# Second band of the first image: direct convolution or minimal filtering form in the prelude

## The chip, the cores and the metric

One Trainium2 chip, one core of it. The metric is the device time of one execution in microseconds, as the median of several runs. A core has TensorE (PE, matrix products into the PSUM banks), VectorE (DVE), ScalarE (ACT), GpSimd (POOL) and SyncE (SP, which here only issues transfers). Each engine works its own queue in order; between engines there are only semaphores.

## What is computed

The input is four images of 64x64 points with 128 channels. Two layers follow each other. In the first, `elu(x)` goes through a 3x3 convolution of 128 to 128 channels, then a 3x3 convolution of 128 to 256, whose halves are combined:

```
c1 = conv_same(jax.nn.elu(x), W1, b1)
c2 = conv_same(c1, W2, b2)
a, b = jnp.split(c2, 2, axis=-1)
c3 = a * jax.nn.sigmoid(b)
```

On `c3` there is a causal attention over the 4096 points with keys of 4 and values of 16 channels ("first attention"); its result, projected by W3, is added to c3 and x. The second layer normalizes each point, does a full attention with 16 heads of 8 channels over the 4096 points ("second attention"), then a feed-forward part and a mixture of two of eight experts. All is float32.

## The kernel before

**Units.** An image is cut into 8 chunks of 512 points (8 image rows) and 4 bands of 16 rows, a band being two chunks. The second attention is a stream of steps: a step takes 128 keys of 4 heads against 512 queries, four score matmuls into two PSUM tiles `s` of 128x1024, two exponentials `e` on ScalarE, and four value matmuls into `acc`. There are three tiles `s`, one bank `acc` and one bank `m` for all other work.

**Order of the work.** The program is written out by Python generators, and what they yield decides the order on each engine; `InOrder` (L104) fixes it as written. Two loops do this. `run_alone` (L1261) is the prelude: it takes one piece of each generator in turn: `convolutions` (L536), `first_attention` (L673), `second_operands_beside` (L832), `fold_and_spread` (L1486) and `spread_beside` (L1497). It ends when the second operands of the first two chunks are there, three tap sets are spread and the first image's two bands are past (`not st.plain`, L1505). After that the main loop lays one attention step per turn, of 1.81 us by the planner's costs, and fills TensorE's rest with pieces of the other generators ("fillers"), while the credit of a turn allows it. The planner's costs are constants in the program.

**The first image's stream.** Its segments come in three groups (`plan`, L1383 on): those that need the operands of 2 chunks (64 steps), of 4 chunks (192 steps) and of all 8. A group cannot start before `batches[b].second`, the count of chunks whose second operands are made, has reached its n; until then no step is written. A chunk's second operands (`second_operands`, L749) are: two projections of the first attention's sums with a division, a normalization (whose power is on GpSimd), a transposition, and the q, v and k projections, each through one bank and written to DRAM; keys and values are read back from there.

**Two forms of the convolution.** The direct form (`first_bands`, L484) takes nine matmuls of 128x512 for each chunk and 128 output channels, one for each tap, accumulated in the bank `m`. The minimal filtering form (`winograd`, L437) makes an output tile of 2x2 from sums of inputs: `row_terms` (L425, four GpSimd operations of 128x528 from a band into `r`) and `col_terms` (L431, one GpSimd operation of 128x1024 for each of four columns, into `v`). For each of the four columns there are then four matmuls of 128x256 with spread taps, in two banks; the first bank is copied out to `sd` (by ScalarE in the prelude, by VectorE later), its halves are added and subtracted (`sums`, `sd`), and the second bank is combined with these. `sd` and `sums` have one buffer each. The spread taps `f_wino1` and `f_wino2` are made in the prelude, by VectorE and, for the gate's half of W2, by GpSimd.

**The bands.** `e_band` holds elu(x) and `c_band` the first convolution's result, two of each, 18 rows with one row of the neighbours on each side. In the first image, bands 0 and 1 go through the direct form, by the loop `for r in range(2)` (L502); bands 2 and 3, and all of the later images, through the minimal filtering form (`jobs`, L612). The direct taps for the gate's half lie in the tile `r`, which `row_terms` takes later (L1296).

Of the kernel before, what the change touches and what calls it, by code (L numbers as in the profile page):

```python
# [9 lines left out]
FP = mybir.dt.float32  # L10
FR = mybir.dt.float32r
AF = mybir.ActivationFunctionType
ALU = mybir.AluOpType
AX = mybir.AxisListType

P = 128
C = 128
IMG = 64
N = IMG * IMG
NT = N // P  # L20
QB = 512
# [105 lines left out]
def fast_path(ctx: ExitStack, tc: tile.TileContext, a: dict, where: dict, out: bass.AP, verdict):  # L127
# [7 lines left out]
    x = a["x"]  # L135
    B = x.shape[0]
    pe, act, sp = (InOrder(tc, e) for e in (nc.tensor, nc.scalar, nc.sync))
# [46 lines left out]
    dve, pool = InOrder(tc, nc.vector, dve_time), InOrder(tc, nc.gpsimd, pool_time)  # L184
# [4 lines left out]
    wk = ctx.enter_context(tc.tile_pool(name="f_wk", bufs=2))  # L189
# [9 lines left out]
    def m_tile():  # L199
        return ps_m.tile([P, QB], FP, tag="m", name="m")  # L200
# [7 lines left out]
    def chunk(tag, name=None):  # L208
        return wk.tile([P, QB], FP, tag=tag, bufs=CHUNKS.get(tag, 1), name=name or tag)
# [10 lines left out]
    def bank():  # L220
        return s_tile()[:, :QB] if alone[0] else m_tile()
# [10 lines left out]
    def load_x(b, c, tag):  # L232
        t = chunk(tag)
        sp.dma_start(out=by_k(t), in_=tb_x[b][:, 4 * c : 4 * c + 4, :])
        return t


    wino1 = const.tile([P, 16, C], FP, name="f_wino1")
    wino2 = const.tile([P, 16, 2 * C], FP, name="f_wino2")

    def row_tile():
        return wk.tile([P, 4 * 8 * (IMG + 2)], FP, tag="r", bufs=1, name="r")

    def taps(src, room=None):

        t = wk.tile([P, 3, 3, C], FP, tag="vg", name="taps") if room is None else room
        for i in range(3):
            act.dma_start(out=t[:, i], in_=src[i].rearrange("kw i o -> i kw o"))
        return t
# [7 lines left out]
    taps1 = taps(a["L0_conv_W1"])  # L257
# [8 lines left out]

    e_band = [const.tile([P, 18, IMG + 2], FP, name=f"f_e_band{i}") for i in range(2)]
    c_band = [const.tile([P, 18, IMG + 2], FP, name=f"f_c_band{i}") for i in range(2)]
    for band in (*e_band, *c_band):
        pool.memset(band[:, :, 0:1], 0.0)  # L270
        pool.memset(band[:, :, IMG + 1 :], 0.0)
    pool.memset(e_band[0][:, 0, :], 0.0)
    pool.memset(c_band[0][:, 0, :], 0.0)

# [63 lines left out]
    def transposed(src, ps):  # L338
        for k in range(4):
            pe.transpose(ps[:, k * P : (k + 1) * P], src[:, k * P : (k + 1) * P], ident)  # L340
# [48 lines left out]
    def rows(ap):  # L389
        return ap.rearrange("p (h w) -> p h w", w=IMG)  # L390
# [4 lines left out]
    COLS = (1, 2, 0, 3)  # L395

    spread_of = []
# [27 lines left out]
    def row_terms(band):  # L425
        r = row_tile().rearrange("p (i y x) -> p i y x", i=4, y=8)
        for i, (x, y, op) in enumerate(SUMS):
            pool.tensor_tensor(r[:, i], band[:, x : x + 15 : 2, :], band[:, y : y + 15 : 2, :], op)
        return r

    def col_terms(r, j):  # L431
        v = wk.tile([P, 4, 8, IMG // 2], FP, tag="v", bufs=4, name="v")
        x, y, op = SUMS[j]
        pool.tensor_tensor(v, r[:, :, :, x : x + 63 : 2], r[:, :, :, y : y + 63 : 2], op)
        return v.rearrange("p i y x -> p i (y x)")
# [45 lines left out]
            late.pop(0)()  # L481
            yield 0.0, "free" if late else "stop"

    def first_bands(st, elu):  # L484


        def nine(taps, band, y, n):
            ps = rows(m_tile()[:, : n * IMG])
            for m in range(9):
                i, j = divmod(m, 3)  # L490
                pe.matmul(
                    ps,
                    lhsT=taps[:, i, j, :],
                    rhs=band[:, y + i : y + i + n, j : j + IMG],
                    start=m == 0,
                    stop=m == 8,
                )
                if m in (2, 5):
                    yield 0.0, "stop"
            return ps  # L500

        for r in range(2):  # L502
            here, there = e_band[r], e_band[1 - r]
            c_here = c_band[r]
            if r == 1:
                pool.tensor_copy(c_here[:, 0, :], c_band[0][:, 16, :])
            for band, y, n, to in (
                (here, 0, 8, slice(1, 9)),
                (here, 8, 8, slice(9, 17)),
                (there, 0, 1, slice(17, 18)),  # L510
            ):
                ps = yield from nine(taps1, band, y, n)
                act.activation(c_here[:, to, 1 : IMG + 1], ps, AF.Identity, bias=b1)
                yield 0.0, "stop"
            st.c3 = wk.tile([P, 2 * QB], FP, tag="c3", bufs=2, name="c3")
            inputs = elu(5 + 2 * r)
            for h in range(2):
                c3, gate = st.c3[:, h * QB : (h + 1) * QB], chunk("sd", "gate")
                ps = yield from nine(taps2a, c_here, 8 * h, 8)
                act.activation(rows(c3), ps, AF.Identity, bias=half_b2a, scale=0.5)  # L520
                next(inputs, None)
                yield 0.0, "stop"
                ps = yield from nine(taps2b, c_here, 8 * h, 8)
                act.activation(rows(gate), ps, AF.Tanh, bias=half_b2[:, 1:2], scale=0.5)
                dve.scalar_tensor_tensor(c3, gate, 1.0, c3, ALU.add, ALU.mult)
                st.done.append(c3)
                next(inputs, None)
                yield 0.0, "stop"
            yield from inputs
        st.plain = False  # L530

    def tiles(ap):

        return ap.rearrange("p (y i) (x h) -> p i y x h", i=2, h=2)

    def convolutions(b, st):  # L536
        xs = list(first_x) if b == 0 else [load_x(b, c, "xe") for c in range(2)]
        yield 0.0, "stop"
        made = [0]

        def elu(n):

            todo = range(made[0], n)
            made[0] = max(made[0], n)
            neg, pos = {}, {}
            for at in range(len(todo) + 2 if todo else 0):
                a_, b_, c_ = (todo[i] if 0 <= i < len(todo) else None for i in (at, at - 1, at - 2))
                if b_ is not None:

                    pos[b_] = chunk("pos")  # L550
                    dve.tensor_scalar(pos[b_], xs[b_], 0.0, None, ALU.max)
                    dve.scalar_tensor_tensor(pos[b_], neg[b_], 1.0, pos[b_], ALU.min, ALU.add)
                    if b_ + 2 < NQ:
                        xs.append(load_x(b, b_ + 2, "xe"))
                if a_ is not None:
                    neg[a_] = chunk("neg")
                    act.activation(neg[a_], xs[a_], AF.Exp)
                if c_ is not None:
                    r, k = divmod(c_, 2)
                    ps = bank()  # L560
                    transposed(pos[c_], ps)
                    put = [(r, slice(1 + 8 * k, 9 + 8 * k), slice(0, 8))]
                    if k == 0 and r > 0:
                        put.append((r - 1, slice(17, 18), slice(0, 1)))
                    if k == 1 and r < 3:
                        put.append((r + 1, slice(0, 1), slice(7, 8)))
                    for band, to, of in put:
                        dve.tensor_scalar(
                            e_band[band % 2][:, to, 1 : IMG + 1], rows(ps)[:, of], -1.0, None, ALU.add
                        )  # L570
                yield (0.0 if c_ is None else 0.6), "free" if at == 0 else "stop"
# [40 lines left out]
        jobs = [(0, 0), (0, 1), (0, 2), (1, 0), (0, 3), (1, 1), (1, 2), (1, 3)]  # L612
        yield from elu(3)
        if b == 0:
            yield from first_bands(st, elu)
            jobs = [(0, 2), (0, 3), (1, 2), (1, 3)]
            while len(spread_of) < 3:
                yield 0.0, "wait"
            yield from elu(7)
        else:  # L620
            pool.memset(e_band[0][:, 0, :], 0.0)
        r_ = row_terms(e_band[jobs[0][1] % 2])
        v = [col_terms(r_, j) for j in COLS]
        yield 0.0, "stop"
        for n, (layer, r) in enumerate(jobs):
# [17 lines left out]
            if layer == 0:  # L643
                yield from winograd(wino1, slice(0, C), v, b1, used, first(r))
                here, above = c_band[r % 2], c_band[(r - 1) % 2]
# [18 lines left out]
            v = ahead  # L664
# [622 lines left out]
    for _ in range(3):  # L1287
        next(batches[0].conv)
    taps2a = taps(a["L0_conv_W2"][:, :, :, :C])
    b1 = const.tile([P, 1], FP, name="f_b1")  # L1290
    act.dma_start(out=b1, in_=a["L0_conv_b1"].unsqueeze(1))
    b2 = const.tile([P, 2], FP, name="f_b2")
    act.dma_start(out=b2, in_=a["L0_conv_b2"].rearrange("(h p) -> p h", p=P))
    half_b2 = const.tile([P, 2], FP, name="f_half_b2")
    half_b2a = half_b2[:, 0:1]
    taps2b = taps(  # L1296
        a["L0_conv_W2"][:, :, :, C:], row_tile()[:, : 9 * C].rearrange("p (i j o) -> p i j o", i=3, j=3)
    )
    for _ in range(2):
        next(batches[0].conv)  # L1300
# [201 lines left out]
    st = batches[0]  # L1502
# [87 lines left out]
    ps = m_tile()  # L1590
# [5 lines left out]
    ps = m_tile()  # L1596
# [703 lines left out]
```

## Time and profile before

| what | us |
|---|---|
| median of 3 runs | 7942.97 (7942.77 to 7944.63) |
| profiled execution | 7943.24 |
| its span | 7941.4 |
| ScalarE busy in the span | 7662.2 |
| TensorE busy in the span | 7753.8 |
| VectorE, GpSimd busy | 4804.7, 671.3 |
| ScalarE's first stream exponential | 159.93 |
| ScalarE without a gap from | 179.05 |

How to read the profile: times are from the start of the span. Nearly all instructions are at L114, since a helper records them, so they are told apart by their tiles: `e<-s` is an exponential, `s<-qx,f_kx` scores of the second attention, `m<-f_e_band,taps` a direct matmul of the first convolution, `m<-v,f_wino` (or `s<-v,f_wino`) one of the minimal filtering form. A float32 matmul has two records. In a timeline a line gives start, length from the first to the last of its instructions, engine, operation, count, and in brackets how long the engine had been idle and what released it. A busy TensorE is modelled, and need not be TensorE at its peak.

### The profile page before, as it was taken

Reading aid. Unit: us, or ns where it says so; the run is one execution under the profiler, and the core shown is the slowest. Engines: PE = TensorE matmul, PEld = TensorE weight load, DVE = VectorE, ACT = ScalarE, POOL = GpSimd, SP = SyncE. Lnnn points to the kernel's source line nnn. Section 1 sums busy time; section 2 is a strip of 40 time slices with the busy share of each in tenths; the row PEclk is TensorE's granted clock in tenths of the full one; section 3 lists DMA queues with packets and bytes.
Section 4 is the critical chain, followed back from the end, with each engine's and each line's share of the span. In section 5 each row is a group of like instructions: output and inputs, shape, how many; then the busy total and the mean of one; then the engine's idle time right before and its main releaser. Section 6 shows DMA issues by size and latency. Waiting matters only on the chain.

```text
span 7941.4 us, 237872 instructions
## 1 busy us (share of the span) xinstructions
PE 7753.8 (98%) x103661; PEld 3284.0 (41%) x103661; DVE 4804.7 (61%) x9290; ACT 7662.2 (96%) x8460; POOL 671.3 (8%) x592
## 2 busy tenths in 40 slices
PE   8999999999999999999999999999999999999998
PEld 3333444444444444444444444444444333333334
DVE  5333556463577666656656776665666666666664
ACT  2999999999999999999999999999999999999996
POOL 2201211000021100000002211000000000000000
PEclk9999999999999999999999999999999999999998
DMA  2112011101100111101010011111111111111221
GB/s 89 62 65 69 24 59 45 59 30 57 35 29 25 39 42 52 44 22 44 27 39 26 26 41 39 52 44 34 32 33 49 49 54 51 50 51 50 73 71 37
DMA packets 334835, 360.96 MB, mean 45 GB/s; under 512 B 148212, under 2 KB 224468, under 8 KB 333780
## 3 DMA queue, kind: packets, MB, share of 16 engines
q1 hardware_dynamic: 329763, 343.87, 13.7%
q8 instruction: 814, 13.34, 0.7%
q10 hardware_dynamic: 4016, 1.77, 0.1%
q14 instruction: 242, 1.97, 0.1%
HBM read 209.50 MB, written 136.05 MB: 44 GB/s over the span
## 4 chain that ended last, share of the span: by engine, by line
PE 44%; issue 2%; DVE 2%; ACT 2%; DMA 0%; POOL 0%; SPq 0%; ACTq 0%; DVEq 0%; POOLq 0%
PE acc L114 22%; PE s L114 13%; PE m L114 9%; ACT e L114 2%; DVE ey L114 1%; DVE h L114 0%; DVE em L114 0%; DVE t L114 0%; DVE eg L114 0%; DVE by_e L114 0%; POOL rs L114 0%; ACT th L114 0%; DVE f_c_band L114 0%; DVE c L114 0%; DMA blocks<-d_y 0%
## 5 line engine op out<-in xcount | busy, mean ns | idle before, releaser
L114 ACT ACTIVATE e<-s 128x1024 f32<-128x1024 f32 x8256 | 7600.8, 1118 | 85.6 <-PE s L114 79.8
L114 PE MATMUL acc<-e,vg 128*9 128x128 f32 (+3 forms) x61840 | 4277.8, 387 | 1.9 <-DVE at L114 1.8
L114 PE MATMUL s<-qx,f_kx 32*128 32x512 f32 (+1 forms) x16512 | 2557.6, 494 | 81.1 <-ACT e L114 59.9
L114 PEld LDWEIGHTS acc<-e,vg 128*9 128x9 f32 x61840 | 1563.0, 90 | 1773.8 <-issue 1206.4
L114 PEld LDWEIGHTS s<-qx,f_kx 32*128 32x128 f32 (+1 forms) x16512 | 1054.3, 182 | 2061.6 <-ACT e L114 1339.7
L114 DVE SCALAR_TENSOR_TENSOR ey<-ey,eg 128x512 f32<-128x512 f32 x1344 | 940.9, 700 | 31.9
L114 DVE COPY at<-acc 128x512 f32<-128x512 f32 x131 | 90.5, 691 | 575.4 <-PE acc L114 572.8
L114 PE MATMUL m<-v,f_wino 128*32 128x256 f32 x5376 | 420.2, 391 | 11.7 <-POOL v L114 7.3
L114 DVE TENSOR_SCALAR ey<-m 128x512 f32<-128x512 f32 x448 | 307.6, 687 | 90.3 <-PE m L114 79.3
L114 DVE SCALAR_TENSOR_TENSOR eg<-em,ey 128x512 f32<-128x512 f32 x448 | 317.0, 708 | 11.4
L114 DVE SCALAR_TENSOR_TENSOR ey<-ey,em 128x512 f32<-128x512 f32 x448 | 316.7, 707 | 9.6
L114 POOL TENSOR_TENSOR rs<-ve,f_minus_half 128x4 f32<-128x4 f32 x64 | 65.2, 1019 | 2989.5 <-DVE ve L114 2957.0
L114 DVE SCALAR_TENSOR_TENSOR ey<-eg 128x512 f32<-128x512 f32 x448 | 312.8, 698 | 0.0
L114 DVE COPY sd<-m 128x512 f32<-128x512 f32 x168 | 115.9, 690 | 307.5 <-PE m L114 307.0
L114 POOL TENSOR_TENSOR v<-r 128x1024 f32<-128x1024 f32 x112 | 219.0, 1961 | 968.0 <-PE m L114 967.5
L114 PE MATMUL m<-f_we,y2T 128*32 128x256 f32 x3968 | 291.9, 388 | 0.0
L114 DVE TENSOR_TENSOR by_e<-m,gates 128x512 f32<-128x512 f32 x248 | 170.3, 687 | 178.9 <-PE m L114 177.8
L114 PE MATMUL m<-hT,f_fw 128*32 128x256 f32 (+1 forms) x2728 | 233.1, 390 | 1.3 <-DVE hT L114 1.2
L114 POOL TENSOR_TENSOR t<-t,h 128x512 f32<-128x512 f32 x32 | 44.4, 1389 | 2243.4 <-DVE h L114 2243.4
L114 DVE TENSOR_TENSOR t<-m,t 128x512 f32<-128x512 f32 x61 | 42.2, 691 | 308.7 <-PE m L114 308.7
L114 DVE TENSOR_SCALAR em<-ey 128x512 f32<-128x512 f32 x448 | 200.4, 447 | 13.7
L114 DVE TENSOR_SCALAR em<-em 128x512 int32<-128x512 int32 x448 | 196.1, 438 | 10.0
(262 smaller groups left out, 4382.6 us busy)
## 6 DMA issues: line engine op xcount, KB each, us to landing
f_kx<-d_k SPq DMA_DIRECT2D x139, 512.0 KB
qx<-d_q SPq DMA_DIRECT2D x152, 256.0 KB
d_q<-two SPq DMA_DIRECT2D x64, 512.0 KB
d_a<-at SPq DMA_DIRECT2D x128, 256.0 KB
vg<-d_v SPq DMA_DIRECT2D x32, 576.0 KB
d_k<-two SPq DMA_DIRECT2D x32, 512.0 KB
d_v<-vc SPq DMA_DIRECT2D x32, 288.0 KB
xe<-in_x_dram SPq DMA_DIRECT2D x32, 256.0 KB
```

The costliest lines, as they stand in the source:

```text
L114: made = op(*args, **kw)
```

## The change

The loop over two bands becomes two generators. `first_band` does band 0 as before, except that the ELUs of chunks 3 and 4 are taken between the first convolution's matmul groups and the first half of layer 2, and that row terms and column terms of band 1 are made by GpSimd after the first half of band 0. `second_band` takes band 1 through `winograd` twice for layer 2 and once for layer 1; row 17 of its first convolution stays direct. Between the two layers it makes the row and column terms of `c_band[1]`. It waits for the three spread tap sets before layer 2. `st.plain` is cleared after layer 2; the ELUs of chunks 5 and 6, which were made during band 1, now come after that. The direct gate taps move from the tile `r` to `c_band[1]`, whose side columns are cleared later for that reason.

```diff
-    for band in (*e_band, *c_band):
+    for band in (*e_band, c_band[0]):
+        clear_sides(band)
...
+    def first_band(st, elu):
+        band, c_to = e_band[0], c_band[0]
+        inputs = elu(5)
+        for here, y, n, to in (
+            (band, 0, 8, slice(1, 9)),
+            (band, 8, 8, slice(9, 17)),
+            (e_band[1], 0, 1, slice(17, 18)),
+        ):
+            ps = yield from nine(taps1, here, y, n)
+            act.activation(c_to[:, to, 1 : IMG + 1], ps, AF.Identity, bias=b1)
+            next(inputs, None)
+            yield 0.0, "stop"
...
+            if h == 0:
+                for _ in inputs:
+                    pass
+                made = row_terms(e_band[1])
+                st.terms = [col_terms(made, j) for j in COLS]
+            yield 0.0, "stop"
+
+    def second_band(st, elu, first, second):
+        here = c_band[1]
+        clear_sides(here)
+        pool.tensor_copy(here[:, 0, :], c_band[0][:, 16, :])
+        yield from winograd(wino1, slice(0, C), st.terms, b1, lambda q: None, first(1))
+        ps = yield from nine(taps1, e_band[0], 0, 1)
+        act.activation(here[:, 17:18, 1 : IMG + 1], ps, AF.Identity, bias=b1)
+        made = row_terms(here)
+        v = [col_terms(made, j) for j in COLS]
+        yield 0.0, "stop"
+        while len(spread_of) < 3:
+            yield 0.0, "wait"
+        st.c3 = wk.tile([P, 2 * QB], FP, tag="c3", bufs=2, name="c3")
+        yield from winograd(wino2, slice(0, C), v, half_b2a, lambda q: None, second(1, False))
+        yield from winograd(wino2, slice(C, 2 * C), v, b2[:, 1:2], lambda q: None, second(1, True))
+        st.done += [st.c3[:, :QB], st.c3[:, QB:]]
         st.plain = False
+        yield from elu(7)
...
         if b == 0:
-            yield from first_bands(st, elu)
+            yield from first_band(st, elu)
+            yield from second_band(st, elu, first, second)
             jobs = [(0, 2), (0, 3), (1, 2), (1, 3)]
-            while len(spread_of) < 3:
-                yield 0.0, "wait"
-            yield from elu(7)
...
     taps2b = taps(
-        a["L0_conv_W2"][:, :, :, C:], row_tile()[:, : 9 * C].rearrange("p (i j o) -> p i j o", i=3, j=3)
+        a["L0_conv_W2"][:, :, :, C:],
+        c_band[1].rearrange("p y x -> p (y x)")[:, : 9 * C].rearrange("p (i j o) -> p i j o", i=3, j=3),
     )
```

## The prediction

> **What bounds the kernel now.** I read the page's busy times first, then busy time by stage, then the timelines of ScalarE and TensorE wherever ScalarE stands still.
>
> ```profile
> PE 7753.8 (98%) x103661; PEld 3284.0 (41%) x103661; DVE 4804.7 (61%) x9290; ACT 7662.2 (96%) x8460; POOL 671.3 (8%) x592
> ...
> L114 ACT ACTIVATE e<-s 128x1024 f32<-128x1024 f32 x8256 | 7600.8, 1118 | 85.6 <-PE s L114 79.8
> ```
>
> 8,256 exponentials of 128x1024. Their mean of 1118 ns counts overlap; their pace is 58.30 us for 64 in the ScalarE timeline from 179.05, 0.91 us each. The stages say where ScalarE is not full (columns: window, length, then busy PE, PEld, DVE, ACT, POOL, clock, DMA share, GB/s):
>
> ```profile
> 0.00:156.00 156.00, 134.50 (x486) 65.48 (x486) 76.89 (x179) 24.34 (x35) 27.40 (x56) 1.00 0.31 94
> 156.00:180.00 24.00, 12.88 (x88) 4.93 (x88) 15.83 (x33) 8.71 (x10) 13.68 (x10) 0.72 0.06 22
> 180.00:324.00 144.00, 139.13 (x1616) 49.86 (x1612) 54.51 (x104) 144.00 (x159) 21.48 (x22) 1.00 0.25 84
> 324.00:334.00 10.00, 4.73 (x40) 1.24 (x40) 0.84 (x2) 1.44 (x3) 9.92 (x7) 0.66 0.04 6
> 334.00:700.00 366.00, 360.76 (x4244) 133.93 (x4248) 136.08 (x301) 366.00 (x404) 33.65 (x30) 1.00 0.18 60
> 700.00:724.00 24.00, 13.47 (x172) 5.63 (x168) 5.96 (x15) 13.59 (x16) 0.00 (x0) 0.79 0.52 167
> ```
>
> The prelude runs to about 156 and TensorE carries it. From 180 on ScalarE carries all, except for two holes, at 324 and at 704. So the time is: when ScalarE becomes continuous, plus its work still open then, plus its holes. The two holes in TensorE's timeline:
>
> ```profile
> 321.43 0.50 PE L114 MATMUL s<-qx,f_kx 32*128 32x512 f32 x4
> 329.27 1.08 PE L114 MATMUL m<-v,f_wino 128*32 128x256 f32 x8 [7.34 <-POOL v L114]
> ...
> 703.03 1.06 PE L114 MATMUL acc<-e,vg 128*9 128x256 f32 x24
> 714.13 0.80 PE L114 MATMUL s<-qx,f_kx 32*128 32x512 f32 x4 [10.04 <-DMA f_kx<-d_k]
> ```
>
> At 703 the stream of attention steps has used up the key blocks of chunks 0 to 3 (256 steps) and needs chunk 7's keys, made just before.
>
> **The change, part by part.**
>
> *TensorE in the second band.* Removed: four times nine matmuls of 128x512 for layer 2 and twice nine for layer 1, 7.96 us for nine (the row at 108.65, two records a matmul), 47.8 us in all. Added: 48 matmuls of 128x256, 0.44 us each (the four of q projection, 1.10 us at 79.58, hold as much), 21.1 us. 26.7 us less on TensorE. But they now form chains.
>
> *The chain in place of it.* I followed the changed kernel's built order from 78.75, where the first band's last gate lands on VectorE, with durations from this trace.
> 1. VectorE up to the second normalization: its listed operations sum to 31.2 us (row pitch: projection set 2.57, normalization 1.89, key set 1.56, three two-term sets of 3.05, here two, 128x256 sums 0.34, bank reads 0.35 and 0.61). Waits on TensorE, GpSimd's power (1.15) and exponentials add some 5. It ends at 115.0. The first layer's band is written at 112.0; row 17 is earlier.
> 2. GpSimd is in order: the power (1.02, as at 112.00) stands before the row terms. Rows 5.17 us (at 155.28), first column term 2.0: 116.1 + 7.2 = 123.3. Nothing of layer 2 can start earlier; TensorE's transposes and projections of chunk 1 queue behind its first matmul.
> 3. Eight steps of layer 2. Each is a bank copy on ScalarE 0.66, sum and difference 0.75, two bank reads 0.80, hand-overs 0.1: 2.3 us, because `sd` and `sums` have one buffer. 18.6 us. Chunk 1's operands lie between on VectorE: 8.2 us. First matmul and last gate: 5. So 123.3 + 31.8 = 155.1: hardly before today, where the last gate is on VectorE at 155.95 to 157.13.
>
> Here a rule speaks against the change. First the row: while GpSimd made terms,
>
> ```profile
> 159.81 0.92 DVE L114 TENSOR_SCALAR w<-u,f_consts 128x512 fp32r<-128x512 f32 x1
> 160.77 2.29 DVE L114 SCALAR_TENSOR_TENSOR qx<-u,f_consts,w 128x512 fp32r<-128x512 f32 x1
> ```
>
> against 0.48 and 0.75 at 56.85 and 57.36, yet the bank read xt (163.37, 0.61) is not longer. The Trainium skill, "SBUF — State Buffer", section "SBUF: two separate sides", says that the pair of ports shared by VectorE and GpSimd is an exclusive lock for a whole instruction, for VectorE operations with two SBUF inputs or in a two-port mode. By the rule, some six operations in my window 123 to 129 wait up to a 2.0 us GpSimd instruction each, +8; by the row, five operations lost 5.2 us in all, and fewer of mine fall inside. I take +2: the stream's first projection starts at 156 to 157 and the first exponential at 157.0. Bounds: -6 (lock never met, early waits hidden) to +8.
>
> *Input terms of the second band.* 13 us of GpSimd, from about 46.5 to 60. GpSimd is idle there until 67 (33.49 us before its memset at 67.27), apart from the bias addition of chunk 0's x, now behind them, at 61 instead of 32.5; its reader is at 61.89. Cost 0; if late by a few us, TensorE's w3f at 71.78 is the next reader, so up to 9 us are covered. The ELUs of chunks 3 and 4 move ahead by one to two matmul groups: the same instructions. The tap tile in c_band[1] moves two memsets and a copy to GpSimd at about 86, 0.7 us, in its idle time.
>
> *What is left undone at 157.* Today, ScalarE is continuous from 179.05 and has by then done 8 exponentials of the stream (7.3), six of chunk 2's first attention (4.9) and two ELU exponentials (1.2): 13.5 us. In the changed kernel these come after 157.0, so the same state is reached at 170.5. At the start, TensorE is slow and the single bank m makes it wait for VectorE's projections of chunk 2; the slow start at 175.95 to 179.05 cost 1.16 us of idle, at 161 to 165 2.6; I take 3 (1 to 6). Gain: 179.05 - 173.5 = 5.5 us.
>
> *The hole at 324.* In the built order two more attention steps now lie between the last layer 1 matmul and the first layer 2 matmul (a segment begins there). Two steps are 3.64 us more cover for the same term making: gain 3.6 (0 to 3.6).
>
> *The hole at 704.* Chunks 2 and 3's first attention and projections are done in the stream now. Everything behind them slips by about 20 steps: chunk 3's keys at step 47 of the 64 that the first segments have (30 before), so no wait there; but chunk 7 is not ready at step 256. In the built order, at that point there follow, without a single stream step between, chunk 7's eight first-attention rounds and all its second operands. The rounds are work ScalarE has anyway; only 1.5 us idle ahead of them. The rest is serial:
> - exponential to copied sums 2.0 (148.19 to 150.21); two projections with their divisions 1.77 each (205.82 to 207.59); normalization to h 4.1 (212.9 to 217.0): 9.6
> - transposes and yT 2.0, q projection 2.05, VectorE's set of it 3.1, v's copy 0.7, k projection 2.05, k's set to the store 1.9: 11.8
> - from the store of keys to the next exponential 13.1 today (701.94 to 715.02). Loads of x now come after the keys, but three ELU exponentials, the third waiting for a reload, stand ahead of it: 14.7, of which 1.9 is work, so 12.8.
>
> 1.5 + 9.6 + 11.8 + 12.8 = 35.7 against 10.4 today (9.78 and 0.62 of ScalarE idle): +25.3. I used slow TensorE durations (1.24 for the transposes at 172.06, after 5.56 idle; 0.60 otherwise). The Trainium skill's "TensorE: Matmul & The Clock Gate", "Part 1", halves the clock after an idle window of about 3.4 us and gives it back only after as long a busy one: by it all three groups are slow, as taken; by the fast rows the sum is 2.6 less. Bounds: 20 to 32.
>
> *Sum.* -5.5 - 3.6 + 25.3 = +16.2 on the span of 7941.4; the profiled execution took 7943.24, 0.3 above the median: 7943.24 + 16.2 = 7959.4, **7960** against 7942.97. After step 256 both orders hold the same work, but for some five steps' shift: ±3.
>
> **Rivals.** A measurement of this kernel can tell 0.2%, 16 us, from no change: 7959.
>
> 1. *The second band goes at TensorE's pace* (the other side). If terms and bank reads hide behind other matmuls, all 26.7 us are gained: the last gate at 157 - 26.7 = 130, 25 before my 155, net 7960 - 25 = 7935. For it: VectorE is only 76.89 of 156 busy. Against it: step 2 alone lets layer 2 start at 123 at the earliest. It decides if the first stream exponential comes before 140.
> 2. *The stall is half as long.* If the late operands of chunk 7 overlap with the rounds, or the keys arrive 10 us earlier: 7950, no change. Against it: m has one bank, and each step reads the one before.
> 3. *The lock costs more.* If each VectorE operation beside GpSimd waits for a whole term, in the first band and in layer 2's start: +8 to +14, 7968 to 7974. For it: the 2.29 row.
>
> **How the numbers follow.** As summed, 7954 to 7967: 0.60, 0.39 of it above 7959. Rival 3: 0.13. Rival 2: 0.15. Rival 1: 0.07. Gains beyond these, such as a stall that goes unnoticed and the fast band together: 0.05. Slower 0.39 + 0.13 = 0.52, same 0.43, faster 0.05. The range takes in rivals 2 and 3: 7944 to 7974; the likeliest case's own is 7954 to 7967.
>
> **What would show it.** First stream exponential at 154 to 160; the first f_wino matmul of layer 2 at 121 to 126; ScalarE's idle at step 256, near 700, of 32 to 40 us in one hole behind DVE and DMA, preceded by eight rounds of first attention; the hole at 324 near 5 us. Wrong if the first stream exponential lies before 150 or the hole near 700 is under 20 us.

## The result, and the profile after

The changed kernel took 7979.8 us in the median (7977.4 to 7980.0), the kernel before 7942.8 (7941.6 to 7944.6) beside it: ratio 1.0044, 95% interval 1.0033 to 1.0056. The predicted time was 7960, its range 7944 to 7974: the direction of the likeliest case was right, the size was not. The profiled span is 7978.0 against 7941.4, +36.6.

The page of the changed kernel, first the busy times, then the group of exponentials (busy time and mean ns, then idle time ahead of them):

```profile
PE 7746.9 (97%) x103829; PEld 3292.5 (41%) x103829; DVE 4834.8 (61%) x9349; ACT 7666.5 (96%) x8468; POOL 703.6 (9%) x611
...
L114 ACT ACTIVATE e<-s 128x1024 f32<-128x1024 f32 x8256 | 7600.1, 1114 | 72.4 <-PE s L114 68.0
```

ScalarE has the same 7600 us of exponentials as before. What grew is its idle time. By stage (columns as before: window, length, busy PE, PEld, DVE, ACT, POOL, clock, DMA share, GB/s):

```profile
0.00:156.00 156.00, 110.21 (x402) 64.26 (x402) 95.30 (x199) 20.85 (x32) 56.90 (x73) 0.89 0.28 87
156.00:180.00 24.00, 16.10 (x134) 6.97 (x136) 11.24 (x29) 14.76 (x18) 0.18 (x1) 0.72 0.08 25
180.00:324.00 144.00, 134.91 (x1680) 53.38 (x1672) 54.25 (x118) 136.07 (x151) 29.51 (x23) 0.96 0.26 86
...
334.00:700.00 366.00, 357.08 (x4224) 130.96 (x4216) 134.84 (x290) 358.88 (x395) 46.88 (x39) 0.99 0.17 55
700.00:724.00 24.00, 16.78 (x135) 5.73 (x132) 6.51 (x24) 14.25 (x16) 0.41 (x1) 0.89 0.06 23
724.00:760.00 36.00, 16.20 (x120) 7.68 (x120) 16.10 (x34) 7.40 (x9) 5.83 (x8) 0.50 0.53 171
```

In the first row TensorE fell from 134.50 to 110.21 us, as it was meant to, and VectorE rose from 76.89 to 95.30. At 180 to 324 ScalarE is no longer full (136.07 of 144, before 144.00), and from 724 to 760 it works 7.40 of 36. Its timeline shows where:

```profile
165.72 3.77 ACT L114 ACTIVATE e<-s 128x1024 f32<-128x1024 f32 x4 [2.97 <-PE s L114]
...
305.11 1.94 ACT L114 ACTIVATE e<-s 128x1024 f32<-128x1024 f32 x2 [5.42 <-PE s L114]
308.10 2.85 ACT L114 ACTIVATE e<-s 128x1024 f32<-128x1024 f32 x3 [1.05 <-PE s L114]
...
376.31 1.94 ACT L114 ACTIVATE e<-s 128x1024 f32<-128x1024 f32 x2 [5.31 <-PE s L114]
...
701.32 7.45 ACT L114 ACTIVATE e<-s 128x1024 f32<-128x1024 f32 x8 [2.21 <-PE s L114]
...
749.17 0.63 ACT L114 ACTIVATE neg<-xe 128x512 f32<-128x512 f32 x1 [33.11 <-DMA xe<-in_x_dram]
```

The first stream exponential comes at 165.72. The hole at 305 is new; the one at 376 is the old one of 324, shortened; the one that ends at 749 is the stall at step 256. In the kernel before, the two holes were these:

```profile
332.59 2.89 ACT L114 ACTIVATE e<-s 128x1024 f32<-128x1024 f32 x3 [8.56 <-PE s L114]
...
715.02 1.94 ACT L114 ACTIVATE e<-s 128x1024 f32<-128x1024 f32 x2 [9.78 <-PE s L114]
```

To add up across kernels I use one yardstick below, the **place**: the time at which ScalarE still has a given amount of attention exponentials to do (summed from busy time in windows of 5 us, interpolated). With 7550 us left, shortly after the prelude, the changed kernel stands at 212.5 and the kernel before at 212.1; with 7100 left (before step 256) at 678.6 and 672.4; with 7040 left (behind it) at 784.9 and 748.0, 36.9 apart, and so to the end. So of the loss nothing had arisen at 212, 6 us lie between there and step 256, 31 at step 256. Each place is read from one profiled execution, and kernels that are the same up to the second band differ by up to 3 us there (below, under "What makes the form slow").

### The profile page after: what moved, and what is told of

Same layout as the page of the kernel before. It is cut to its first block, busy times and chain, and to the rows that moved or that the text cites. A ratio compares the mean times of both kernels' runs of the same rounds, so it can differ in the third digit from the quotient of the medians.

```text
span 7978.0 us, 238308 instructions
## 1 busy us (share of the span) xinstructions
PE 7746.9 (97%) x103829; PEld 3292.5 (41%) x103829; DVE 4834.8 (61%) x9349; ACT 7666.5 (96%) x8468; POOL 703.6 (9%) x611
## 4 chain that ended last, share of the span: by engine, by line
PE 43%; issue 3%; DVE 2%; ACT 2%; POOL 0%; DMA 0%; SPq 0%; ACTq 0%; DVEq 0%; POOLq 0%
PE acc L114 22%; PE s L114 12%; PE m L114 9%; ACT e L114 2%; DVE ey L114 1%; DVE h L114 0%; DVE em L114 0%; DVE t L114 0%; DVE eg L114 0%; DVE by_e L114 0%; DMA blocks<-d_y 0%; POOL rs L114 0%; POOL v L114 0%; POOL xt L114 0%; SPq L114 0%
```

## The experiments

Two theories went into them. **T**: chunk 2's and 3's operands, which no longer fit into the prelude, come too late in the stream. **R**: the filtering form's chain in the prelude is what costs.

**Deferral alone, in the kernel before.**

```diff
-            while alone[0] and st.second < c - 1:
+            while alone[0] and (st.second < c - 1 or (b == 0 and c == 2)):
```

> The kernel before, with one condition more: chunk 2's first attention waits until the prelude has ended, so it and all behind it goes into the stream. No minimal form, no term of GpSimd in the prelude. In the built order chunk 3's keys come at step 47 (30 before), chunk 7's at step 256 without a step between (253 before). Theory T (the loss is work that no longer fits into the prelude and finds no turn in the stream in time): hole at step 256 about 36 us instead of 10.4, a second hole near 305 of 6 us for keys loaded at the segment's start; the prelude ends up to 4 earlier: 7942.8 + 26 + 6 - 3 = 7972 (7967 to 7977). Rival R (the loss is the filtering form's chain in the prelude, the terms, the port, the slow TensorE): nothing of that is here, so 7943 or less (7936 to 7946).

Measured 7964.0 (7960.0 to 7967.6), ratio 1.0025 (1.0016 to 1.0035), span 7960.6. ScalarE's timeline of it:

```profile
144.23 5.61 ACT L114 ACTIVATE e<-s 128x1024 f32<-128x1024 f32 x6 [0.18 <-PE s L114]
155.78 29.79 ACT L114 ACTIVATE e<-s 128x1024 f32<-128x1024 f32 x33 [5.94 <-PE s L114]
...
284.54 1.94 ACT L114 ACTIVATE e<-s 128x1024 f32<-128x1024 f32 x2 [4.68 <-PE s L114]
...
727.10 0.63 ACT L114 ACTIVATE neg<-xe 128x512 f32<-128x512 f32 x1 [31.62 <-DMA xe<-in_x_dram]
```

Both holes of the changed kernel are there without a single minimal form in the second band: T is right about them. Its time, 7967 to 7977, lay above the measured 7964.0 and R's 7943 below it. The place of 7550 is why: it is at 193.6, 18.5 us earlier than before, where T allowed up to 4. So chunk 2's first attention, squeezed into the prelude, was what held the kernel before back, and the direct second band is over at 145. The changed kernel defers the same work and starts at 165.7. Its form *loses* 18.9 us (212.5 - 193.6) against the direct form with the same deferral; the equal places of before and after hide a gain and a loss of the same size. R is right too; a third experiment, "Chunk 2's first attention back in the prelude", tests this reading. (Of b_defer's +19.2 in the span, 14.1 are there behind step 256; the rest accrues later in gaps under 1 us, which I did not trace.)

**One free turn instead of two**, in both kernels. (A free turn is one at the start of a segment in which the main loop adds no filler.)

```diff
-                quiet[0] = kt < seg.lo + 2 and at > 0 and not late
+                quiet[0] = kt < seg.lo + (2 if batches[0].second == NQ else 1) and at > 0 and not late
```

> The changed kernel, whose stream leaves one turn at a segment's start free of fillers instead of two while the first image's operands are being made. Chunk 7's keys come at step 242 instead of 256, chunk 3's at 37 instead of 46. T: the hole of 38 us at step 256 goes, the one of 6.5 at 305 stays (37 is behind step 32, from which those keys could be fetched ahead): 7979.8 - 38 = 7942 (7938 to 7948). R: the prelude is unchanged and so is most of the loss: 7975 to 7980.

> The same edit in the kernel before: chunk 7's keys at step 227 instead of 253, chunk 3's at 27. T: only its own hole of 10.4 us goes: 7932.5 (7930 to 7936), so this and the changed kernel with the same edit differ by the prelude (+1.6), the hole at 305 (+6.5) and the hole behind it (-2.6), some 5 to 10 us, not by 37. R: the difference between the two kernels stays near 37, whatever the turns.

Measured: a_quiet1 7971.5 (7966.3 to 7975.4), b_quiet1 7958.8 (7950.7 to 7964.1), the latter 1.0017 (1.0010 to 1.0024) of before. Both expectations of T missed, and R's too: it had a_quiet1 at 7975 to 7980 and the two kernels 37 apart, and they are 12.7 apart. The stall did go: in a_quiet1 4.14 and 1.82 us of idle are left around step 256. But with 7150 us left a_quiet1 is at 648.9 against 628.4, b_quiet1 at 641.9 against 622.4: the 20 us were lost on the way, 2 to 3 of them before the second band already. What TensorE waited for from 180 to 700, first before, then b_quiet1 (total us, times, longest):

```profile
PE m L114 <- POOL v L114: 7.3, 1, 7.3
PE s L114 <- ACT e L114: 7.0, 23, 0.4
```

```profile
PE acc L114 <- DVE at L114: 13.8, 14, 2.4
PE m L114 <- POOL v L114: 7.3, 1, 7.3
```

At a segment's end VectorE copies `acc` out, and the next segment's values need that bank. With two free turns the kernel before has no such wait in its list; with one, a filler's VectorE work can stand ahead of that copy. So 13.8 of the 20 us have a name. A free turn is not spare room; T's remedy was wrong, not its finding.

**Keys fetched as soon as they are ready.**

```diff
                     if later.ready():
                         key_quarter(later, quarters[0])
+                    else:
+                        wanted.append((later, quarters[0]))
...
+                for item in [w for w in wanted if w[0].ready()]:
+                    key_quarter(*item)
+                    wanted.remove(item)
```

> The changed kernel, where a key quarter that was not ready when its place came free is fetched as soon as it is ready, instead of at the start of the segment that reads it. The order of all other work is the same. T: the hole of 5.42 and 1.05 us at 305 goes, nothing else: 7979.8 - 6 = 7973.5 (7972 to 7976). R: no change if that hole is TensorE's own slow start and not the keys: 7979 to 7980.

Measured 7975.2 (7973.5 to 7978.6), span 7976.8. This is as T expected (7972 to 7976). The hole is gone; ScalarE's line across it:

```profile
294.32 25.87 ACT L114 ACTIVATE e<-s 128x1024 f32<-128x1024 f32 x28
```

With 7350 us left it stands at 421.9, 5.6 earlier than the changed kernel, though 1.6 later at 7550, where its edit has not acted yet. At the end 1.2 us by the span and 4.6 by the medians remain. The cause of the hole is shown, the gain of its removal only roughly.

**One layer at a time.** Direct second layer (with the same deferral), then direct first layer:

```diff
-        yield from winograd(wino2, slice(0, C), v, half_b2a, lambda q: None, second(1, False))
-        yield from winograd(wino2, slice(C, 2 * C), v, b2[:, 1:2], lambda q: None, second(1, True))
+        for h in range(2):
+            ps = yield from nine(taps2a, here, 8 * h, 8)
+            ps = yield from nine(taps2b, here, 8 * h, 8)
...
-        yield from winograd(wino1, slice(0, C), st.terms, b1, lambda q: None, first(1))
+        for h in range(2):
+            ps = yield from nine(taps1, e_band[1], 8 * h, 8)
```

> The minimal form for the second band's first layer alone; its second layer direct, at TensorE's pace, and chunk 2's first attention kept out of the prelude, so that as much is deferred as in the changed kernel and in b_defer. (Layer 2's second tap tile gets room of its own, which the experts' weights take over after the prelude.) Read at the place where ScalarE has 7550 us of attention exponentials left: 193.6 us in b_defer, 212.5 in the changed kernel. The chain theory C (each layer's form costs time because of its waits, TensorE standing idle): half of the 19 us here, last gate at 153, that place at 203; the rest of the loss is as in the changed kernel, with 3 to 6 us more at step 256 because chunk 7's first attention begins there: 7973 (7968 to 7978). The rival L (only the second layer's terms on GpSimd cost): the place at 194 to 198, 7962 to 7966.

> The minimal form for the second band's second layer alone; its first layer direct, no terms of GpSimd before it. The same work is deferred. C: the first layer's rows are there at 107, the first matmul of layer 2 in the form at 115 to 118 instead of 125.2, the last gate at 154 instead of 162.8, the place of 7550 us left at 203; 7969 (7965 to 7973). L: no better than the changed kernel, the place at 210 to 213, 7976 to 7980.

Measured: a_layer1d 7979.2 (7968.6 to 7984.0), place of 7550 at 202.9; a_layer2 7967.1 (7965.4 to 7967.9), place 200.2. Against b_defer's 193.6 the first layer's form costs 9.3, the second's 6.6; 15.9 of the 18.9. C holds: both layers cost, though not half each. The medians fit less well for a_layer1d, whose 7979.2 lies above the expected 7968 to 7978 (it scatters, and chunk 7's first attention starts only at step 256 there); I rest on the places. The length of the second band, from the first band's last gate to its own, says the same more sharply. In b_defer these are

```profile
77.39 0.69 DVE L114 SCALAR_TENSOR_TENSOR c<-gate,c 128x512 f32<-128x512 f32 x1 [1.96 <-ACT gate L114]
...
144.09 1.19 DVE L114 SCALAR_TENSOR_TENSOR c<-gate,c 128x512 f32<-128x512 f32 x1 [8.23 <-ACT gate L114]
```

and in the changed kernel

```profile
78.14 0.69 DVE L114 SCALAR_TENSOR_TENSOR c<-gate,c 128x512 f32<-128x512 f32 x1 [1.96 <-ACT gate L114]
...
161.28 1.54 DVE L114 SCALAR_TENSOR_TENSOR c<-t,c 128x256 f32<-128x256 f32 x4
```

To the end of the last gate that is 67.9 us direct and 84.7 in the form; a_layer1d has 78.6, a_layer2 73.4. The first layer's form adds 10.7 and the second's 5.5, 16.2 of 16.8 together.

**Chunk 2's first attention back in the prelude**, in the changed kernel.

```diff
-        lambda: st.second >= plan[0].n and len(spread_of) == 3 and not st.plain,
+        lambda: st.second >= plan[0].n and len(st.ready) >= 3 and len(spread_of) == 3 and not st.plain,
```

> The changed kernel, whose prelude goes on until chunk 2's first attention is done, as in the kernel before: the fourth corner beside before (direct, chunk 2 in the prelude), b_defer (direct, chunk 2 in the stream) and the changed kernel (minimal form, chunk 2 in the stream). If the two terms add up: the place of 7550 us left at 212.5 + 18.5 = 231 (225 to 233); the hole at step 256 20 to 24 instead of 38, because chunk 7's queries come at step 254 and only v, keys and the way through DRAM are left; the hole at 305 stays (keys at step 36, behind 32): 7978 + 18 - 16 = 7980 (7974 to 7986). If the form needs no deferral to be as fast (the deferral alone is the loss): 7955 to 7962.

Measured 7977.5 (7976.8 to 7979.6), place 229.9. ScalarE's timeline:

```profile
173.06 3.77 ACT L114 ACTIVATE e<-s 128x1024 f32<-128x1024 f32 x4 [9.94 <-PE s L114]
...
189.76 5.61 ACT L114 ACTIVATE e<-s 128x1024 f32<-128x1024 f32 x6 [10.19 <-PE s L114]
...
750.89 0.63 ACT L114 ACTIVATE neg<-xe 128x512 f32<-128x512 f32 x1 [17.44 <-DMA xe<-in_x_dram]
```

Two serial waits of 10 us in the prelude for 18 us less at step 256: no change in sum. So the four corners are:

| second band | chunk 2's first attention | place of 7550 | idle at step 256 | span |
|---|---|---|---|---|
| direct (before) | prelude | 212.1 | 10.4 | 7941.4 |
| direct (b_defer) | stream | 193.6 | 33.9 | 7960.6 |
| filtering (a_ready3) | prelude | 229.9 | 19.8 | 7977.3 |
| filtering (after) | stream | 212.5 | 38.2 | 7978.0 |

Down the column of places, the form costs 18 to 19 us with and without the deferral, and the deferral brings 17 to 18.5 with either form. In the span they do not add: the deferral costs 19.2 us with the direct form and 0.7 with the other, and the form alone, without the deferral, costs 35.9. Both then end in late operands: a_ready3 also keeps the hole for chunk 3's keys (4.72 and 1.05 us) and has 9.4 us more idle at step 256 than the kernel before.

**What makes the form slow.** Layer 2's terms by VectorE; four buffers for `sd`; more VectorE work:

```diff
-        made = row_terms(here)
-        v = [col_terms(made, j) for j in COLS]
+        made = row_terms(here, dve)
+        v = [col_terms(made, j, dve) for j in COLS]
...
-            sd = chunk("sd")
+            sd = chunk("ey", "sd") if alone[0] else chunk("sd")
...
+                    for half in range(2 if alone[0] else 0):
+                        dve.tensor_copy(t[:, half * QB // 2 : (half + 1) * QB // 2], t[:, half * QB // 2 : (half + 1) * QB // 2])
                     used(q)
```

> The changed kernel, with the terms of the second band's second layer (four of rows, four of columns) made by VectorE instead of GpSimd. If GpSimd's pace and its hold on VectorE's port are what makes the chain long: the first matmul of layer 2 at 121 to 123 instead of 125.2, the four operations of h back to some 1.1 us from 4.7, the place of 7550 left at 206 to 209, 7972 to 7975. If VectorE's own queue is the limit, 7 us of terms more on it eat that up: the place at 212 to 217, 7977 to 7983.

> The changed kernel, with four buffers instead of one for sd, the bank copy of the filtering form, in the prelude (sums keeps its one). If the pitch of 2.3 us a step is the wait of the next bank copy for that buffer, 16 steps fall towards VectorE's own 1.6 to 1.9: the place of 7550 left at 205 to 209, 7971 to 7975. If it is VectorE's order: the place at 211 to 213, 7976 to 7979.

> The changed kernel with 24 additional copies of 128x256 on VectorE in the second band's filtering form, two after each of the twelve pairs of bank reads (each copies a buffer onto itself): some 0.25 us each, 6 us of VectorE and nothing else. If VectorE's queue sets the prelude's end (65.90 us busy of the 84.25 from 78.75 to 163.00): the place of 7550 us left moves from 212.5 to 216.5 to 218.5, 7982 to 7984. If the hand-overs between the engines do, and VectorE's copies fit into its 18 us of gaps: the place at 212.5 to 214, 7978 to 7979.

Measured: a_tdve 7981.9 (7977.4 to 7982.4), place 212.8; a_sd2 7980.7 (7976.3 to 7984.1), place 213.0; a_dve2 7986.7 (7981.9 to 7990.1), place 216.7. In a_tdve VectorE's timeline is

```profile
121.81 1.11 DVE L114 TENSOR_SCALAR h<-xt,mv,rs 128x128 f32<-128x128 f32 x4 [1.13 <-POOL rs L114]
122.84 2.56 DVE L114 TENSOR_TENSOR r<-f_c_band 128x528 f32<-128x528 f32 x4
125.43 4.63 DVE L114 TENSOR_TENSOR v<-r 128x1024 f32<-128x1024 f32 x4
```

where the changed kernel, with GpSimd making these, has

```profile
118.48 4.71 DVE L114 TENSOR_SCALAR h<-xt,mv,rs 128x128 f32<-128x128 f32 x4 [1.13 <-POOL rs L114]
127.95 1.17 DVE L114 TENSOR_TENSOR sums<-sd 128x256 f32<-128x256 f32 x1 [4.76 <-ACT sd L114]
129.15 2.03 DVE L114 TENSOR_TENSOR sd<-sd 128x256 f32<-128x256 f32 x1
```

`h` is back to 1.11, the place unchanged: VectorE now spends 7.2 us on the terms itself. But the place hides something here. The first band, which these edits don't touch, ends later in some of the profiles: its last gate is at 78.14 in the changed kernel and 78.06 in a_dve2, but at 80.38 in a_tdve, 80.65 in a_sd2 and 80.66 in a_keys. In a_keys, whose program is the same up to the stream, TensorE's mean clock from 66 to 81 was 0.89, in the changed kernel 1.00. Counted from that gate, a_tdve's second band is shorter:

```profile
80.38 0.69 DVE L114 SCALAR_TENSOR_TENSOR c<-gate,c 128x512 f32<-128x512 f32 x1 [1.96 <-ACT gate L114]
...
160.70 1.54 DVE L114 SCALAR_TENSOR_TENSOR c<-t,c 128x256 f32<-128x256 f32 x4
```

It takes 81.9 us to the end of the last gate, against 84.4 to 84.9 in the five profiles with this band unedited (after, a_keys, a_ready3, a_plan6, a_quiet1). So taking the terms from GpSimd wins some 2.8 us of the 16.8, and a_sd2, at 83.5, some 1.2: both far less than was expected of them. In the changed kernel a step's pitch is 2.29 us (`sums` at 144.09, 146.37, 148.66). Two things fit it equally: the loop through the bank copy, and VectorE's own five operations. Without the wait for the buffer it is still 2.18 (in a_sd2 at 146.79, 148.97, 151.16). In a_dve2 the group of added copies

```profile
L114 DVE COPY t<-t 128x256 f32<-128x256 f32 x24 | 5.8, 286 | 0.0
```

is 5.8 us busy (the 286 ns of each overlap), and the band takes 88.0 us, 3.4 more; the place moves by 4.2. So some 60 to 70% of what is put on VectorE comes out at the end. VectorE's time in these chains is most of the path, and waiting for others the rest. (Each copy stands ahead of an operation that reads its `t`, so the run doesn't tell VectorE's queue from the chain that runs through it.) The stage says the same, b_defer from 78.75 to its last gate, then the changed kernel to its own:

```profile
78.75:144.00 65.25, 63.47 (x233) 32.10 (x231) 35.52 (x87) 8.45 (x13) 3.14 (x6) 1.00 0.35 120
```

```profile
78.75:163.00 84.25, 48.93 (x211) 35.53 (x211) 65.90 (x141) 12.54 (x20) 21.81 (x19) 0.77 0.26 92
```

Direct, TensorE is busy 63.47 of 65.25 us at full clock and VectorE 35.52. In the form, VectorE is busy 65.90 of 84.25, TensorE 48.93 at a mean clock of 0.77. Of the 65.90, 7.9 are operations stretched beside GpSimd: `h`, and two pairs of `sums` and `sd`. That leaves 22.5 more than direct; at 60% this would make 13.5 of the 16.8 us, which is an estimate from a_dve2 and no measurement. The bound has moved, and the new one is higher. What TensorE's slow groups contribute, no run isolates.

**A version meant to beat both**: blocks of 2, 4, 6 and 8 chunks, so that step 256 needs only chunks 4 and 5. In the changed kernel; in b_defer with the keys' edit; then with one tile left to VectorE in segments of 24 tiles too; then with the pieces' pace set to end earlier.

```diff
-        for n in (2, 4, NQ) if b == 0 else (NQ,):
+        for n in (2, 4, 6, NQ) if b == 0 else (NQ,):
...
-            self.beside = (20,) if hi - lo == NT else ()
+            self.beside = (20,) if hi - lo >= 24 else ()
...
-            rate = (sum(part[1] for part in fillers) + later) / max(40, sum(steps_left) - 160)
+            rate = (sum(part[1] for part in fillers) + later) / max(40, sum(steps_left) - 260)
```

> The changed kernel, whose first image is attended in blocks of 2, 4, 6 and 8 chunks instead of 2, 4 and 8: after step 256 come steps over chunks 4 and 5, and chunk 7's keys are needed only some 300 steps later. In the built order they come at step 277. The stall theory (the 38 us at step 256 are one serial chain that nothing covers): it goes, 7978 - 38 and up to 8 for 24 more segment starts and 16 more partial sums: 7940 to 7948. The rival, total TensorE work (what is not done in the stall has to be paid in the turns, as with one free turn instead of two, where 36 us of hole went and only 8 us came back): 7965 to 7975.

> The kernel before with chunk 2's first attention kept out of the prelude (as b_defer), the blocks of 2, 4, 6 and 8 chunks (as a_plan6), and keys fetched as soon as they are ready (as a_keys): no minimal form in the second band. If the 18.5 us that b_defer wins in the prelude, the 34 us of its hole at step 256 and the 5.7 of its hole at 285 are separate terms: 7960.6 - 34 - 6 = 7921, and up to 8 for the additional segments: 7921 to 7930, faster than both kernels. By the rival, total TensorE work: 7945 to 7955.

> As d_p6keys (7951.3, with 14 us of exponentials more on ScalarE than the kernel before, because only segments over all 32 key tiles leave one tile to VectorE), but segments over 24 tiles leave one to VectorE too. The 16 exponentials come back: ScalarE's attention exponentials 7601 instead of 7615 us and the time 7951 - 14 = 7937 (7934 to 7945), if VectorE and the accumulators keep up; 7950 or more if TensorE then waits for VectorE at the segments' ends, as with one free turn in the kernel before (13.8 us there).

> As d_p6keys (7951.3), with the pace of the pieces between the steps set to end 260 steps before the last step instead of 160. In the kernel before the last exponential ends 66.5 us before the end, in d_p6keys 79.8, because chunk 6's closing work is unfinished there. If that is all: 7951.3 - 13 = 7938 (7935 to 7943), no slower than the kernel before; if the pieces crowd the stream instead: 7950 or more.

Measured: a_plan6 7978.3 (7975.3 to 7979.6); d_p6keys 7952.2 (7947.7 to 7956.9), 1.0012 (1.0005 to 1.0019) of before; d_p6b 7963.8 (7958.3 to 7968.2); d_p6t260 7960.8 (7957.3 to 7964.9). a_plan6's ScalarE across step 256, then its exponentials on the page:

```profile
689.21 71.14 ACT L114 ACTIVATE e<-s 128x1024 f32<-128x1024 f32 x78
```

```profile
L114 ACT ACTIVATE e<-s 128x1024 f32<-128x1024 f32 x8272 | 7616.9, 1121 | 77.8 <-PE s L114 72.6
```

The stall of 38 us is gone, but the time, 7978.3, is above what either theory expected (7940 to 7948, and 7965 to 7975). At the last exponential the kernel is 16.7 us ahead with 16.8 us of exponentials more behind it, so 33.5 of the 38 had stayed won: the stall was the serial chain, and not TensorE time that has to be paid later. What the blocks cost I had not counted: 16 exponentials more (16.8 us), and 81.3 instead of 66.7 us from the last exponential to the end. -38.2 + 16.8 + 14.6 = -6.8; the span says -2.1.

d_p6keys in the same way from b_defer's 7960.6: -33.9 - 5.7 + 16.1 + 12.5 = -11.0, that is 7949.6, measured 7951.3. The expected 7921 to 7930 missed by these two costs; that 7952.2 lies in the rival's 7945 to 7955 is not for the rival's reason, by this sum.

Giving the 16 exponentials back to VectorE (d_p6b) raised ScalarE's wait for scores by 25 us (page: 69.3 in d_p6keys, here 94.7), as its second case expected: TensorE's `acc` waits 14.5 us, 8 times, for VectorE. And a faster pace of pieces (d_p6t260) restored the closing 66.5 but lost 25 on the way (with 1000 left 6888.9 against 6863.3):

```profile
L114 ACT ACTIVATE e<-s 128x1024 f32<-128x1024 f32 (+1 forms) x8256 | 7601.7, 1113 | 94.7 <-PE s L114 90.9
```

No version beat the kernel before.

## Why the prediction was wrong, step by step

- **Step 1, TensorE -26.7.** Against the direct form with the same deferral it is 63.47 - 48.93 = 14.5, with the form's matmuls on a slower clock. (I misread the row at 79.58: four records are two matmuls. The 0.44 stands, as half of a matmul of 128x512.) It did not decide: TensorE was no longer the bound.
- **Step 2, the chain: the failing step.** The first half was near: normalization at 117.3 (115.0), first layer 2 matmul at 125.16 (123.3). From there to the last gate I had 31.8 and it took 37.6, and the first exponential is at 165.72 instead of 157.0. Of these 8.7 us, 1.9 are the later start; some 2.3 are collisions with GpSimd, 4.3 where I took 2; some 2 are slow matmul groups, which I put at nothing; and 2.9 lie between the last gate (162.82) and the first exponential, for which the sum held nothing at all, although in the kernel before it is 2.8 (157.13 to 159.93). (These are estimates from the rows; they make 9.1.) The pitch of 2.3 us a step came out, in part by luck: I had left VectorE's fifth operation (0.69) out, and it runs beside the bank copy. TensorE's timeline in the changed kernel:

```profile
88.58 2.05 PE L114 MATMUL s<-v,f_wino 128*128 128x256 f32 x4 [5.57 <-DVE f_v L114]
...
125.16 2.08 PE L114 MATMUL s<-v,f_wino 128*128 128x256 f32 x4 [11.70 <-POOL v L114]
...
145.68 7.03 PE L114 MATMUL s<-v,f_wino 128*128 128x256 f32 x24 [2.71 <-DVE t L114]
...
162.88 2.08 PE L114 MATMUL s<-c,f_rwq 128*128 128x256 f32 x4 [7.90 <-DVE c L114]
```

  TensorE waits for the other engines each time. After these waits its first groups of four often take 2.05 to 2.08 us; at other times they take 1.03 to 1.13. The groups at 125.16, 131.93 (the q projection) and 162.88 each hold up the next engine by some 1 us. I took slow durations at step 256 but none here.
- **The lock.** I weighed the exclusive lock in the Trainium skill, "SBUF — State Buffer", "SBUF: two separate sides", against the row of 2.29 us and took +2; by the rule it was +8. `h`'s four operations took 4.71 us instead of 1.11 (hidden behind the terms), and two pairs of `sums` and `sd` 3.20 and 2.76 instead of 0.84. All together that is 7.9, close to the rule's 8, but only 4.3 of it lie in the chain, nearer to my 2. It isn't the main cause of the loss: a_tdve removes the first of these collisions, puts 7.2 us of terms on VectorE instead, and wins 2.8. What the lock alone costs, no run shows.
- **Step 3, the work left over.** From the first exponential to the state of 179.05 it took 15.0 us (180.7 - 165.7), predicted 16.5. Right; so the gain of 5.5 became a loss of 1.6 by step 2 alone.
- **Step 4, the old hole.** 5.31 and 0.63, 5.9, in the place of 8.56; predicted 5.0, so the gain is 2.6 instead of 3.6.
- **Step 5, "so no wait there": the second failing step.** I compared step 47 with step 64, where the keys are used. They are *fetched ahead* at step 32, when their place comes free, and only if they are ready then (30 before, 46 now). Otherwise they are asked for when the segment that reads them starts, at 297.70, and TensorE's scores wait 5.17 us:

```profile
297.70 1.19 SPq L114 DMA_DIRECT2D f_kx<-d_k  x2
...
304.22 0.80 PE L114 MATMUL s<-qx,f_kx 32*128 32x512 f32 x4 [5.17 <-issue]
```

  The profile names no releaser; that it is the keys, a_keys shows, where the wait is gone. The cost was put at nothing and is 5.42 and 1.05 us of ScalarE.
- **Step 6, the hole at step 256.** 38.2 against 35.7: 2.7 (2.21 and 0.48) instead of 1.5 ahead of the chain, 20.7 from the end of the rounds to the store of keys against 21.4, and from there to the next exponential 14.7 of idle instead of 12.8. The structure was right, and transposes and projections were slow as taken (1.15 and 1.93 to 1.94). This agrees with what I took from the Trainium skill, "TensorE: Matmul & The Clock Gate", "Part 1", a clock halved after some 3.4 us of idle and given back after as long a busy stretch: the transposes come after 4.49 us idle, and waits of 0.79 to 1.11 us break up the work behind them. Of the gaps behind the hole (1.40, 3.58 and 0.56 us; before 2.88 and 0.73), 1.9 us are new; later nothing changed, as said.

Together: 7.1 us from step 2; 8.9 between 180 and 700 (13.9 of idle in place of 8.56 - 3.6: 6.5 for the keys, 1.5 in new gaps at 275, the rest a smaller gain at the old hole); 2.5 from the hole at step 256 and 1.9 from the gaps behind it. That is the 20.4 between +16.2 and +36.6.

Of the rivals, TensorE's pace (7935) fell at 165.7, the stall half as long (7950) at 38.2. The lock costing more was true in its rows and too small. A case that I had not on the list held: the chain 8.7 us late, and one transfer asked for late.

What I misread more deeply is the comparison in step 2, "hardly before today". Today's last gate at 155 was late because chunk 2's first attention ran between the matmuls of the band, not because of TensorE's 7.96 us per nine: b_defer's direct band ends at 145.3, with TensorE busy nearly throughout. I weighed the new chain against a number that contained work which the change moves away.

## What to carry to other kernels

When a change moves work out of a stage as well as speeding it up, first work out what the moving alone does with the old code, or try it: gain and loss can cancel at one point and the bill arrives in another stage. A form that trades TensorE work for sums trades it onto VectorE; add up VectorE's whole queue in that stage (here 35.5 us became 65.9, stretched operations included) before counting matmuls. For data that moves later, look for the moment at which its transfer is *asked for*, not only for the one at which it is read.

## What was not expected of the hardware

This stage, in which TensorE waits often, was slowed twice: of the 26.7 us of matmul time that the form saves, some 12 did not appear in a stage whose mean clock was 0.77 (1.00 in the direct one; the two windows hold nearly, not exactly, the same other work). GpSimd took 4.70 and 7.71 us for the four row and four column terms, VectorE 2.56 and 4.63 for the same operations. The same program isn't clocked the same each time: with no edit in reach, the first band ended at 78.1 us in some profiles and at 80.4 to 81.1 in others, with a clock of 0.89 where it was 1.00. In a_keys the slow stretch began after only 1.58 us of idle (`acc` at 67.09 takes 3.37 us in place of 2.50). And an engine's turn without a piece was doing something: with one of the two filled, TensorE waited 14 times for VectorE's copy of `acc`, 13.8 us in all.
